# More buffers for edge loads, dense one-hots and a new dealing of edge sums in a graph network

## The chip, the cores and the metric

The kernel runs on one core of one Trainium2 chip, in one launch. The time is device microseconds (us) of that core for one execution, inputs and outputs in the chip's memory (DRAM). A time is the median of several runs. The profile comes from one execution of its own.

## What is computed

Two layers of a graph network over 6,250 nodes with 128 features and 200,000 edges that are sorted by their destination:

```python
edge_index = jnp.stack([src, dst])
h = jnp.maximum(_layernorm(x, axis=-1), 0.0)
# layer 0
agg_src = jax.ops.segment_sum(h[src], dst, num_segments=N_NODES)
agg_edge = jax.ops.segment_sum(edge_features, dst, num_segments=N_NODES)
x = x + relu(concatenate([h, agg_src, agg_edge], axis=1) @ W.T + b)
# layer 1: two mean aggregations
h = jnp.maximum(_layernorm(x, axis=-1), 0.0)
h = relu(segment_mean(h[src], dst) @ W1_l + b1 + h @ W1_r)
x = x + relu(segment_mean(h[src], dst) @ W2_l + b2 + h @ W2_r)
```

(segment_mean stands for the sum of the messages divided by the larger of the number of edges and 1.) All inputs and outputs are float32.

## The kernel before

The kernel never gathers a node's row by its index. It first **builds** a dense matrix of counts, how often node s is the source of an edge into node d, as bfloat16 in DRAM (counts_d). Then each of the three aggregations is a dense product of that matrix with the node features. The features go in as three bfloat16 terms that sum to the float32 value (terms). The change lies in the build alone.

**Groups, tiles, units.** The 200,000 edges are cut in 196 groups (G) of 1,024: 128 partitions by U = 8 tiles. Since the edges are sorted by destination, a group touches a narrow window of destination nodes, and since the destinations are drawn unevenly, the window widens as the groups go on. REGIONS holds 14 rows for 14 groups each (RUN): tiles per unit n (4, 2 or 1), nodes of a unit's window w, groups per stretch k, nodes of a ring sw, and nodes of a group's window for the edge sums win (8 to 74). Two regions have n = 4 (28 groups), four have n = 2 (56 groups), eight have n = 1 (112 groups). A **unit** is n tiles that share one window.

**Counts.** For each group VectorE makes two kinds of one-hot matrices in onehots (L391): sp, one column per source's place in its block of 128, and sq, one column per pair of destination in the window and source block (NB = 49 blocks, so NB*w columns). Each has two buffers (pool hots). PE multiplies them tile by tile into a PSUM tile pu (L534), which has three buffers. For n = 1 a second, small matmul (L546) with the one-hot sc adds the tile before, where windows overlap. ScalarE then evicts each unit from pu into a ring in SBUF (L561 for n = 1; L556 and L566 for n > 1), at a place that it reads from a register. For n > 1 GpSimd adds the first 49 columns of a unit into the ring (L564). When a stretch of groups is done, SP writes the ring to counts_d (L584). Three rings take turns.

**Edge sums.** The same groups also give agg_edge. edge_sums(g) has SP load the group's edge features, 512 KB (edge_t, L426, pool edges with 3 buffers). VectorE makes a one-hot hot (L428) of win columns for each of 8 tiles, in one of three padded buffers whose rows are 128 wide. PE multiplies each tile of features with the 128 columns of that row (L437) into a PSUM tile pe with two buffers. VectorE adds the first win columns into aggE at the group's first node (L442), which it reads into a register. The matmuls are float32, and the trace has two PE passes for each.

**The order of the work.** PE's order is written out. After each unit or pair of units of counts, sum_edges lets the edge tiles run up to a place, and a manual dependency puts the next edge matmul behind the counts before it:

```python
spent += share(n) * len(units) / len(live)
sum_edges(min(int(spent / shares * GU + 0.5), GU), counted)
```

share(n) is the weight of a group of counts; GU = 1568 edge tiles are dealt in proportion to it. SP takes all loads and most stores of the build in one queue, in the order that the program gives: edge loads, chunks of x for the layer norm (x_c, L476), rows of the first product (r_d, L352), and the writes of the ring (L584). A load for which no buffer is free, or a write whose ring is not complete, holds up all that stands behind it. Every third group the first layer norm and product of one block of 128 nodes (first_layer, L341 to L351) is fitted in.

Of the kernel before, what the change touches and what calls it, by code (L numbers as in the profile page):

```python
# [9 lines left out]
F32 = mybir.dt.float32  # L10
# [10 lines left out]
P = 128  # L21
D = 128
U = 8
# [29 lines left out]
WINMAX = 74  # L53
# [3 lines left out]
def kernel(ctx: ExitStack, tc: tile.TileContext, x, srcl, dstl, edge, w0t, b0, w1l, b1, w1r, w2l, b2, w2r, out):  # L57
# [11 lines left out]
    nc = tc.nc  # L69
# [55 lines left out]
    build = ExitStack()  # L125
# [47 lines left out]
    for key, t in [*pick.items(), *pick_l.items()]:  # L173
        n = key if isinstance(key, int) else key[0]
        e = 16 * n
# [186 lines left out]

    rings = build.enter_context(tc.tile_pool(name="rings", bufs=1))
    hots = build.enter_context(tc.tile_pool(name="hots", bufs=2))
    edges = build.enter_context(tc.tile_pool(name="edges", bufs=3))

    ring_of = [rings.tile([P, SWMAX * NB], BF16, name=f"ring{i}") for i in (2, 1)]

    padded = [rings.tile([P, U, P], F32, name=f"hot{i}") for i in range(2)]
    ring_of.append(rings.tile([P, SWMAX * NB], BF16, name="ring0"))  # L370
    padded.append(rings.tile([P, U, P], F32, name="hot2"))
    ring_of.reverse()
    padded.reverse()
    for t in ring_of[:1] + padded + ring_of[1:]:
# [3 lines left out]
    def value(ap, engine, most):  # L378
        return nc.values_load(
            ap, engines=[engine], min_val=0, max_val=most, skip_runtime_bounds_check_because="clamped on the chip"  # L380
        )
# [39 lines left out]
    def edge_sums(g):  # L421

        win = win_of(g)
        e = edges.tile([P, U, D], F32, name="edge_t")
        at_e = min(g * EG, E - EG)
        nc.sync.dma_start(e, edge[at_e : at_e + EG, :].rearrange("(p u) f -> p u f", u=U))  # L426
        hot = padded[g % len(padded)]
        nc.vector.tensor_tensor(  # L428
            hot[:, :, :win],
            iota[:, :win].unsqueeze(1).to_broadcast([P, U, win]),  # L430
            rel[:, g, :].unsqueeze(2).to_broadcast([P, U, win]),
            op=ALU.is_equal,
        )
        ps = bpsum.tile([P, 512], F32, name="pe", bufs=2)
        for u in range(U):
            behind = yield
            mm = nc.tensor.matmul(ps[:, :P], e[:, u, :], hot[:, u, :], start=u == 0, stop=u == U - 1)  # L437
            if behind is not None:
                tc.add_manual_dep(mm.ins, behind.name, IN_ORDER, reason="in turn with the counts")
        base = value(first_i[0:1, g : g + 1], ET.DVE, N - 1)  # L440
        to = aggE[:, bass.ds(base, win)]
        nc.vector.tensor_tensor(to, to, ps[:, :win], op=ALU.add)  # L442

    def all_edge_sums():
        for g in range(G):
            yield from edge_sums(g)
# [37 lines left out]
        return products(0, b, h, terms[0], pu[:, :P], pu[:, 512 : 512 + 2 * D], nc.sync)  # L484


    share = lambda n: 1.0 if n > 1 else 2.0
    shares = sum(share(n) * ng for _, ng, n, *_ in stretches)
    spent = 0.0
    before = None  # L490
# [5 lines left out]
    for si, (g0, ng, n, w, k, sw, win) in enumerate(stretches):  # L496
# [7 lines left out]
        for g in range(g0, g0 + ng):  # L504
# [21 lines left out]
            for j in range(0, len(live), many):  # L526
                units = live[j : j + many]
                pu = bpsum.tile([P, 2 * 512], F32, name="pu", bufs=3)
                for i, t0 in enumerate(units):
                    for t in range(t0, t0 + n):  # L530
                        c = i * 512
                        while c < i * 512 + nq:
                            z = min(c // 512 * 512 + 512, i * 512 + nq)
                            mm = nc.tensor.matmul(  # L534
                                pu[:, c:z],
                                sp[:, t, :],
                                sq[:, t, c - i * 512 : z - i * 512],
                                start=t == t0,
                                stop=t == t0 + n - 1 and (n > 1 or c > i * 512),
                            )  # L540
                            c = z
                    if n == 1:

                        slot = t0 + 1 if t0 != live[0] else 1
                        for j0, (sp_b, t) in enumerate(last_tiles):
                            mm = nc.tensor.matmul(  # L546
                                pu[:, i * 512 : i * 512 + NB],
                                sp_b[:, t, :],
                                sc[:, slot + 1 - len(last_tiles) + j0, :NB],
                                start=False,  # L550
                                stop=j0 == len(last_tiles) - 1,
                            )
# [207 lines left out]
    for b in order:  # L760
# [10 lines left out]
        n = P if b + 1 < NB else last  # L771
# [231 lines left out]
```

## Time and profile before

| | us |
|---|---|
| median of 3 runs | 2244.61 (2238.09 to 2248.94) |
| the profiled execution | 2237.15 |
| its span | 2235.4 |
| PE busy in the span | 2073.7 (93%) |
| VectorE busy | 1242.0 (56%) |
| ScalarE busy | 789.2 (35%) |
| GpSimd busy | 205.0 (9%) |
| groups of counts with n = 4 | from 34 us |
| with n = 2 | from 106.5 us |
| with n = 1 | from 310.5 us |
| end of the build | 911.5 us |

In the rows of the profile PE is the tensor engine's matmuls, PEld its weight loads, DVE VectorE, ACT ScalarE, POOL GpSimd, SP SyncE; a q behind a name is the engine's sequencer, which issues, loads registers and waits. L437 is line 437 of the kernel. A row of a group reads: line, engine, operation, tile written <- tiles read, shape, xcount | busy us in all, mean ns of one | idle us of the engine just before them <- what ended most of it. A row of waits reads: who <- for whom: us in total, times, longest. A row of the timeline reads: start us, us, engine, line, operation, tiles, xcount [idle before <- releaser]. Matmuls overlap in a pipeline, so the time of a run of them is read from the start of the first to the start of the next instruction. The granted clock is the share of full speed that PE was given.

### The profile page before, as it was taken

What the parts mean: (1) busy time and instruction counts of PE and PEld (TensorE: products, weight loads), DVE (VectorE), ACT (ScalarE), POOL (GpSimd) and SP (SyncE); (2) the same over time, 40 slices, a digit from 0 to 9 for tenths busy, and PEclk for the clock granted to TensorE, in tenths of its full rate; (3) what the DMA queues carried; (4) which work ended last, traced back from release to release, by engine and by line L of the source; (5) the groups of instructions that cost most, each with busy time, mean ns of one, the idle gap of its engine ahead of it and who ended that gap; (6) DMA issues with size and microseconds to landing.
All of it is one profiled execution on the core that took longest, in us unless ns stands there. A gap on an engine that the chain in (4) does not pass through costs nothing.

```text
span 2235.4 us, 38803 instructions
## 1 busy us (share of the span) xinstructions
PE 2073.7 (93%) x13717; PEld 1691.1 (76%) x13717; DVE 1242.0 (56%) x2419; ACT 789.2 (35%) x2011; POOL 205.0 (9%) x427
## 2 busy tenths in 40 slices
PE   6977778899999999689999999999999999999998
PEld 5865567677776677478878887788888888888887
DVE  8987776577777777465555554544444431111111
ACT  3465566688888889211111111111111110000000
POOL 4576650000000000100000000000000000000000
PEclk9999999999999999899999999999999999999999
DMA  3555566678888778745555555555555556666663
GB/s 121 179 191 173 193 221 233 217 266 280 281 301 300 283 293 291 280 167 205 205 194 203 206 205 189 190 194 206 192 190 201 202 187 227 226 226 227 227 226 135
DMA packets 147226, 488.20 MB, mean 218 GB/s; under 512 B 16017, under 2 KB 86735, under 8 KB 127312
## 3 DMA queue, kind: packets, MB, share of 16 engines
q1 hardware_dynamic: 88452, 456.84, 56.9%
q10 hardware_dynamic: 57996, 27.16, 4.2%
q8 instruction: 111, 1.82, 0.3%
q0 software_dynamic: 576, 1.63, 0.2%
q14 instruction: 91, 0.75, 0.1%
HBM read 362.19 MB, written 123.38 MB: 217 GB/s over the span
## 4 chain that ended last, share of the span: by engine, by line
PE 60%; ACT 13%; DMA 9%; DVE 8%; issue 6%; ACTq 2%; POOLq 0%; SPq 0%; POOL 0%; DVEq 0%
PE ps L609 44%; ACT ring L561 10%; PE pe L437 6%; PE pu L534 5%; DMA counts_d<-ring 4%; DMA c<-counts_d 3%; PE pz L344 2%; ACTq L384 1%; DMA edge_t<-in_edge 1%; DVE sq L391 1%; DVE worse L618 1%; PE pt L341 1%; DVE high L617 1%; ACT h L334 1%; DVE sp L391 1%
## 5 line engine op out<-in xcount | busy, mean ns | idle before, releaser
L609 PE MATMUL ps<-terms,c 128*128 128x384 bf16 (+1 forms) x7203 | 1226.7, 327 | 16.9 <-DMA c<-counts_d 16.9
L609 PEld LDWEIGHTS <-c 128*128 128x128 bf16 x7203 | 1019.9, 142 | 183.6 <-issue 21.7
L437 PE MATMUL pe<-hot,edge_t 128*128 128x128 f32 x3136 | 521.0, 294 | 33.5 <-DMA edge_t<-in_edge 17.1
L561 ACT CAST ring<-pu 128x490 f32 (+6 forms) x891 | 469.5, 534 | 96.9 <-PE pu L546 43.0
L437 PEld LDWEIGHTS pe<-hot,edge_t 128*128 128x128 f32 x3136 | 418.2, 195 | 70.2 <-issue 18.1
L534 PE MATMUL pu<-sq,sp 128*128 128x512 bf16 (+7 forms) x1782 | 387.0, 313 | 55.9 <-ACT ring L561 26.7
L391 DVE TENSOR_TENSOR sq<-iota,q_e 128x3136 bf16<-128x3136 f16 (+8 forms) x196 | 353.5, 1804 | 102.4 <-PE pu L546 83.2
L620 DVE TENSOR_REDUCE y<-ps 128x128 f32<-128x384 f32 x147 | 81.2, 552 | 383.3 <-PE ps L609 383.3
L534 PEld LDWEIGHTS <-sp 128*128 128x128 bf16 x1782 | 175.6, 100 | 99.4 <-issue 33.6
L564 POOL TENSOR_TENSOR ring<-ring,fore 128x49 f32 x280 | 161.8, 578 | 102.3 <-ACT fore L556 36.1
L618 DVE TENSOR_REDUCE worse<-high 128x1 f32<-128x3136 bf16 x49 | 167.5, 3419 | 1.6
L546 PE MATMUL pu<-sc,sp 128*128 128x49 bf16 x892 | 163.1, 186 | 0.0
L347 DVE TENSOR_TENSOR r<-pz,b_sb 128x128 f32<-128x128 f32 x98 | 28.6, 292 | 225.0 <-ACT terms L345 225.0
L391 DVE TENSOR_TENSOR sp<-iota,p_e 128x1024 bf16<-128x1024 f16 x196 | 135.4, 691 | 21.8 <-PE pu L534 16.9
L546 PEld LDWEIGHTS <-sp 128*128 128x128 bf16 x892 | 87.0, 98 | 70.2 <-issue 38.5
L566 ACT CAST ring<-pu 128x196 f32 (+5 forms) x280 | 112.3, 403 | 67.9 <-issue 39.5
L330 ACT ACTIVATE rstd<-mv,eps 128x1 f32<-128x1 f32 x98 | 29.5, 301 | 291.1 <-DVE mv L328 291.0
L757 ACT ACTIVATE h<-y 128x128 f32<-128x128 f32 x49 | 15.2, 309 | 281.0 <-DVE y L749 281.0
L617 DVE TENSOR_TENSOR high<-c 128x3136 bf16<-128x3136 bf16 x49 | 87.6, 1789 | 42.1 <-DMA c<-counts_d 42.1
L428 DVE TENSOR_TENSOR hot<-iota,rel 128x64 f32<-128x64 f16 (+13 forms) x196 | 96.5, 493 | 0.0
L351 DVE TENSOR_TENSOR terms<-z,terms 128x128 bf16<-128x128 f32 x147 | 43.9, 299 | 59.5 <-ACT terms L350 59.0
L350 ACT CAST terms<-z 128x128 bf16<-128x128 f32 x147 | 44.0, 299 | 76.4 <-DVE z L349 75.6
(144 smaller groups left out, 867.3 us busy)
## 6 DMA issues: line engine op xcount, KB each, us to landing
c<-counts_d SPq DMA_DIRECT2D x147, 1568.0 KB, 6.1
edge_t<-in_edge SPq DMA_DIRECT2D x196, 512.0 KB, 4.2
counts_d<-ring SPq DMA_DIRECT2D x21, 735.0 KB, 3.8
counts_d<-ring SPq DMA_DIRECT2D x14, 1004.5 KB, 5.4
counts_d<-ring SPq DMA_DIRECT2D x14, 931.0 KB, 4.7
counts_d<-ring SPq DMA_DIRECT2D x14, 882.0 KB, 4.6
counts_d<-ring SPq DMA_DIRECT2D x14, 833.0 KB, 4.9
own<-r_d ACTq DMA_DIRECT2D x147, 64.0 KB, 5.3
```

The lines of the kernel that those rows point to most:

```text
L391: nc.vector.tensor_tensor(to.rearrange("p t (c two) -> p t c two", two=2), iota[:, :m].rearrange("p (c two) -> p c two", two=2).unsqueeze( ...
L428: nc.vector.tensor_tensor(hot[:, :, :win], iota[:, :win].unsqueeze(1).to_broadcast([P, U, win]), rel[:, g, :].unsqueeze(2).to_broadcast([P ...
L437: mm = nc.tensor.matmul(ps[:, :P], e[:, u, :], hot[:, u, :], start=u == 0, stop=u == U - 1)
L534: mm = nc.tensor.matmul(pu[:, c:z], sp[:, t, :], sq[:, t, c - i * 512 : z - i * 512], start=t == t0, stop=t == t0 + n - 1 and (n > 1 or c ...
L546: mm = nc.tensor.matmul(pu[:, i * 512 : i * 512 + NB], sp_b[:, t, :], sc[:, slot + 1 - len(last_tiles) + j0, :NB], start=False, stop=j0 == ...
L561: nc.scalar.copy(ring[:, bass.ds(to_put[t0], nq)], pu[:, i * 512 : i * 512 + nq])
L564: add = nc.gpsimd.tensor_tensor(to, to, fore[:, i, :], op=ALU.add)
L566: put = nc.scalar.copy(ring[:, bass.ds(to_put[t0 // n] + NB, nq - NB)], pu[:, i * 512 + NB : i * 512 + nq])
L609: nc.tensor.matmul(ps[:, :m], stands, moves, start=i == 0, stop=i == len(products) - 1)
L617: nc.vector.tensor_tensor(high, cf[:, :half], cf[:, half:], op=ALU.max)
L618: nc.vector.tensor_reduce(worse[:, 6 + b : 7 + b], high, AX.X, ALU.max)
L620: nc.vector.tensor_reduce(y, ps[:, : NK * D].rearrange("p (k f) -> p f k", k=NK), AX.X, ALU.add)
```

## The change

Three things change in the build.

1. The pool of the edge loads has five buffers in place of three.
2. The one-hots for the edge sums are written close together: tile u stands at column u*win in place of u*128. A matmul still reads 128 columns; those past its own win belong to the next tile, and the sums in them are not used, as only the first win columns of the result are added to aggE. A buffer shrinks from 1,024 to 646 float32 columns.
3. The weights by which edge tiles are dealt to the groups of counts are 1.0, 1.5 and 1.75 for units of four, two and one tiles, in place of 1.0, 1.0 and 2.0.

```diff
-    edges = build.enter_context(tc.tile_pool(name="edges", bufs=3))
+    edges = build.enter_context(tc.tile_pool(name="edges", bufs=5))
...
-    padded = [rings.tile([P, U, P], F32, name=f"hot{i}") for i in range(2)]
+    HP = U * WINMAX + P - WINMAX
+    HP += HP % 2
+    padded = [rings.tile([P, HP], F32, name=f"hot{i}") for i in range(2)]
     ring_of.append(rings.tile([P, SWMAX * NB], BF16, name="ring0"))
-    padded.append(rings.tile([P, U, P], F32, name="hot2"))
+    padded.append(rings.tile([P, HP], F32, name="hot2"))
...
         nc.vector.tensor_tensor(
-            hot[:, :, :win],
+            hot[:, : U * win].rearrange("p (u w) -> p u w", w=win),
             iota[:, :win].unsqueeze(1).to_broadcast([P, U, win]),
             rel[:, g, :].unsqueeze(2).to_broadcast([P, U, win]),
             op=ALU.is_equal,
...
-            mm = nc.tensor.matmul(ps[:, :P], e[:, u, :], hot[:, u, :], start=u == 0, stop=u == U - 1)
+            mm = nc.tensor.matmul(ps[:, :P], e[:, u, :], hot[:, u * win : u * win + P], start=u == 0, stop=u == U - 1)
...
-    share = lambda n: 1.0 if n > 1 else 2.0
+    share = lambda n: {4: 1.0, 2: 1.5, 1: 1.75}[n]
```

## The prediction

> **What bounds the kernel now.** I read the page's slices first: from 960 us on PE is busy nine tenths and no line of the change runs there. The change acts in the build, which ends at 911.5 us. I cut the build where the number of tiles per unit changes, by the starts of VectorE's one-hots: groups 0 to 27 (units of four) from 34 us, 28 to 83 (units of two) from 106.5, 84 to 195 (units of one) from 310.5; the last stage once more at 463, because two different engines limit its parts, and at 749.5, where a unit's columns no longer fit 512. Columns: stage, length, busy time of PE, weight loads, VectorE, ScalarE, GpSimd, granted clock, DMA share, GB/s.
>
> ```profile
> 34.00:106.50 72.50, 66.04 (x523) 57.91 (x524) 65.37 (x155) 33.33 (x122) 39.36 (x60) 0.95 0.57 186
> 106.50:310.50 204.00, 158.80 (x1077) 124.19 (x1075) 163.75 (x328) 119.22 (x428) 136.53 (x232) 0.96 0.54 186
> 310.50:463.00 152.50, 127.70 (x1038) 107.32 (x1037) 97.91 (x238) 100.00 (x281) 7.74 (x19) 0.96 0.68 233
> 463.00:749.50 286.50, 268.16 (x2086) 204.91 (x2084) 220.88 (x372) 247.95 (x501) 0.20 (x1) 1.00 0.82 289
> 749.50:911.50 162.00, 152.51 (x1245) 115.36 (x1244) 120.33 (x154) 140.57 (x226) 1.77 (x1) 0.99 0.79 287
> ```
>
> In the two-tile stage no engine is full: PE 78%, VectorE 80%, GpSimd 67%. From 463 us PE looks full at 94%, but ScalarE's own timeline says otherwise. Eight evictions take 5.1 us, each batch starts about 0.15 us after the last, and a group lasts 5.25 us:
>
> ```profile
> 795.65 5.09 ACT L561 CAST ring<-pu 128x539 f32 x8 [0.15 <-issue]
> 800.90 5.10 ACT L561 CAST ring<-pu 128x539 f32 x8 [0.16 <-PE pu L546]
> 806.15 5.10 ACT L561 CAST ring<-pu 128x539 f32 x8 [0.15 <-issue]
> ```
>
> So past 463 us the evictions are the bound. What they still wait for, in the table of waits from 463 to 911.5 us, is all that a relieved PE or DMA can give back there, 31 us of 448:
>
> ```profile
> ACT ring L561 <- DMA counts_d<-ring: 15.7, 15, 2.6
> ACT ring L561 <- PE pu L546: 15.1, 24, 1.6
> ```
>
> Next the chain that ended last, cut to the two-tile stage (its listed steps are start, length, what):
>
> ```profile
> 194.33 5.18 DMA edge_t<-in_edge
> ...
> 263.78 5.30 DMA edge_t<-in_edge
> ```
>
> and the same places in PE's timeline, with one at 318 to 324 us and one at 392 to 398 us, and an undisturbed run of eight edge matmuls for comparison:
>
> ```profile
> 178.59 0.77 PE L437 MATMUL pe<-hot,edge_t 128*128 128x128 f32 x2 [3.36 <-DMA edge_t<-in_edge]
> ...
> 199.56 0.79 PE L437 MATMUL pe<-hot,edge_t 128*128 128x128 f32 x2 [3.08 <-DMA edge_t<-in_edge]
> ...
> 269.22 2.05 PE L437 MATMUL pe<-hot,edge_t 128*128 128x128 f32 x8 [5.22 <-DMA edge_t<-in_edge]
> ...
> 323.94 0.91 PE L437 MATMUL pe<-hot,edge_t 128*128 128x128 f32 x6 [3.50 <-DVE st L326]
> ...
> 397.69 0.77 PE L437 MATMUL pe<-hot,edge_t 128*128 128x128 f32 x2 [3.23 <-DMA edge_t<-in_edge]
> ...
> 704.39 1.14 PE L437 MATMUL pe<-hot,edge_t 128*128 128x128 f32 x8
> ```
>
> Five times PE stands for 3 to 5 us for a late edge tile (18.4 us in sum; at 323.94 the label names VectorE, but the two edge loads had only been issued at 318.5 and 319.9). The loads are late because SP is one queue: in the two-tile stage its counts writes (L584) waited 65.8 us for GpSimd's last ring add, and the edge loads stand behind them, at most three buffers ahead.
>
> **Five buffers.** The five stalls go, 18.4 us of PE idle. After each, the trace shows the clock halved: eight edge matmuls took 2.05 us after the 5.22 us stall against 1.14. Counting the slow work behind each, about 2 us more per stall, 10 in all. A rule bears on this: the Trainium skill, "TensorE: Matmul & The Clock Gate", HAM oscillation, says that idle gaps above some 3.4 us put PE at half clock. By the rule only the 5.22 and the 3.50 us stalls would cost (4 us of slow work, as an estimate); by the rows the 3.08 and 3.23 us ones did as well. I take the rows: 10.
>
> In the built order SP's edge loads run 5 to 7 tiles ahead of PE instead of 3 to 5. In groups 112 to 194 each counts write stands behind an edge load whose buffer comes free on average 28 PE instructions (weight loads counted) after the group's last matmul; before it was 40. So the ring is written out earlier, and the 15.7 us of ring waits should shrink, not grow.
>
> **Shares.** 28, 56 and 112 groups have units of four, two and one. The weights summed to 28 + 56 + 224 = 308; now to 28 + 84 + 196 = 308. So the first stage keeps its 17.8 edge groups of 196, the second goes from 35.6 to 53.5, the last from 142.5 to 124.7: 17.8 edge groups move. Each is 16 PE passes (two for each float32 matmul). Eight took 0.97 us at 704.39, the next count matmul starting at 705.36: 1.94 us a group, 34.6 us of PE work moved. On VectorE each brings a one-hot and an add,
>
> ```profile
> L428 DVE TENSOR_TENSOR hot<-iota,rel 128x176 f32<-128x176 f16 x13 | 4.9, 393 | 0.0
> L442 DVE TENSOR_TENSOR aggE<-aggE,pe 128x22 f32 x10 | 1.7, 168 | 0.5 <-PE pe L437 0.5
> ```
>
> 0.56 us, 10.0 us in all. The 17.8 moved edge loads are 9.3 MB, 46 GB/s more over 204 us: 232, below the 289 that the later stage sustains.
>
> Two-tile stage. PE's busy time becomes 158.8 + 34.6, less 6 of slow clock (three of the stalls are here), 187. How full PE can run is unknown here. The bounds are the neighbours: 84% as at 310 to 463 us, which still has stalls, and 94% as after 463: 223 or 199 us. I take 87%, what the 310 stage has once its two stalls (6.7 us) and slow clock are taken out of both sides ((127.7 - 4) / (152.5 - 6.7 - 4)): 215 us, **+11**, stalls already credited. VectorE is then at 174 of 215, not the bound. The aggE add stands in VectorE's queue ahead of the next groups' sp and sq and waits for PE's last edge matmul; it waited 26.8 us for 109 sums after 463 us, 0.25 us each, so 4 us for 17.8 more, inside the 87%.
>
> 310 to 463 us. A quarter of the moved groups, 4.45 x 1.94 = 8.6 us of PE, and 4 of slow clock go: 115 us of PE at 87% is 132. ScalarE's work (100 us and its register loads) is then near; I take 135, **-17** (bounds 132 and 142, the stalls alone).
>
> 463 to 911.5 us. The remaining 26 us of PE work are taken out of a stage that ScalarE paces, so nearly all of it becomes PE idle. Of the 31 us of waits I take 12: half the waits for PE, under a third of those for the ring. **-12**, bounds 0 and -25. If evictions did not cover it, the full 26 would return.
>
> The first stage and all that follows the build are as before: 0.
>
> **Dense one-hots.** The write keeps its element count. Matmuls now read 128 columns from row starts at multiples of 4 x window bytes, not 512. The count one-hots already start each tile 588 bf16 columns, 1176 bytes, after the last, no multiple of 512 either, and four of their matmuls of 441 columns pass in 0.91 us, of which one alone is 0.36: 183 ns each, 2.4 columns a ns: taken as 0. Bound above: 4 ns on each of 3136, 12 us. The three memsets of L375 shrink by 378 columns before the first one-hot, some 1 us, beside the first edge load, for which PE waits until 38.5 us.
>
> A rule speaks against the move: the Trainium skill, "SBUF — State Buffer", Who interferes with whom: a VectorE instruction with two SBUF inputs holds the port that GpSimd reads through, and the other blocks for the whole instruction. The moved one-hots have two SBUF inputs and enter the stage where GpSimd adds into the ring (L564). By the rule, 17.8 x 0.39 = 7 us more for GpSimd. The trace has L564 at 273 ns when alone and up to 1.9 us beside sq, which agrees; beside a hot alone four of them took 270 to 282 ns, which does not. I take 0 here and leave the 7 to a rival.
>
> **Sum.** +11 - 17 - 12 = -18. The profiled execution took 2237.15 us (span 2235.4), so 2219; the median of the runs is 2244.61, 7.5 more, and I put the change on that: **2227**.
>
> **Rivals.** A change of 0.5%, 11 us, is about what a measurement of this kernel can tell from none: below 2233 is faster, above 2256 slower.
>
> *ScalarE gives nothing back.* If after 463 us only 3 us return, since evictions pace the stage, the 310 stage stops at -12 because ScalarE fills up there too, and two tiles cost +13, the sum is -2: 2243, no change. For it: batches 0.15 us apart. Against: the 31 us of listed waits and the stalls.
>
> *The two-tile stage pays in series (slower).* PE runs in a written order, so an added edge tile stands between a unit's matmuls and the next unit. If the rounds PE, ScalarE, GpSimd, VectorE leave no room, PE's 34.6, VectorE's 10 and the port's 7 add up: 51.6, less 9 for the stalls (half of the stage's 11.7 idle and 6 slow, as the other engines use such time), +43, against -29 later: +14, 2259. For it: 45 us of PE idle there, much of it waits for ring evictions, in gaps of 1 to 2 us. Against: eight more passes fit in 1 us. It decides from a stage length of 233 us (204 + 29).
>
> **How the numbers follow.** Forecast 0.63, its own range 2207 to 2233 (the bounds above, not all at one end); nothing back 0.20; in series 0.15; dense reads that cost 0.02. Under 2200 all three terms would have to reach their best bound (-5 - 21 - 25), and above 2256 the series case holds most: low 2200, high 2256. Faster 0.65, same 0.20, slower 0.15.
>
> **What would show it.** Right: edge matmuls of 17.8 groups more between the starts of groups 28 and 84; no PE idle above 2.5 us behind an edge load and fewer half-clock stretches; two-tile stage near 215 us, units of one near 572 in place of 601; ScalarE's waits for PE and ring after 463 us near 19 us. Wrong: two tiles at 230 or more; group periods after 463 us unchanged; stalls of PE that now name VectorE or GpSimd in place of the load; edge matmuls above 0.97 us for eight.

## The result, and the profile after

The changed kernel takes **2222.22 us** (median of 5 runs, 2206.9 to 2225.29) against 2244.61 before (2238.09 to 2248.94): the ratio is 0.9895, 95% interval 0.9871 to 0.9920, some 22 to 24 us faster. The forecast was 2227 us, faster.

The profiled execution of the changed kernel took 2206.9 us, its span 2205.2. That is the fastest of its five runs, so its span is 30 us shorter than before, not 22 to 24. The stages were cut at the same groups as before, 28, 84 and 112, and once more at 168 (the columns are those of the prediction's first fence):

```profile
34.00:106.40 72.40, 65.90 (x523) 57.83 (x524) 65.36 (x155) 33.38 (x122) 39.26 (x60) 0.95 0.61 199
106.40:307.00 200.60, 181.86 (x1356) 153.05 (x1355) 170.13 (x357) 120.85 (x428) 137.92 (x230) 0.99 0.68 233
307.00:445.40 138.40, 118.94 (x989) 99.32 (x988) 98.48 (x238) 102.19 (x285) 9.83 (x22) 0.96 0.73 252
445.40:727.80 282.40, 253.44 (x1928) 187.05 (x1927) 216.80 (x353) 243.96 (x498) 0.20 (x1) 1.00 0.76 273
727.80:884.50 156.70, 148.65 (x1173) 106.08 (x1172) 117.61 (x146) 140.05 (x228) 1.77 (x1) 1.00 0.75 278
```

Read the second line against the one before: 279 more PE matmuls in the two-tile stage and 23 us more of PE busy time, in a stage that is 3.4 us *shorter*, at 99% of the clock in place of 96%. GpSimd's busy time is as it was, 138 us. DMA moved 233 GB/s there (forecast 232).

The chain of work in that stage has no step on an edge load any more; its longest steps are:

```profile
144.86 2.57 issue
171.83 2.12 ACTq L387
210.89 2.46 PE pe L440 x22
293.90 2.24 ACTq L387
301.98 2.07 issue
```

After group 112, the table of waits has for ScalarE:

```profile
ACT ring L564 <- PE pe L440: 11.3, 13, 1.4
ACT ring L564 <- PE pu L549: 10.1, 15, 1.5
...
ACT ring L564 <- DMA counts_d<-ring: 5.9, 10, 1.7
```

The waits for the ring fell from 15.7 to 5.9 us. Those for PE did not fall, they rose from 16 to 21 us. And a new long stop stands in PE's timeline at the start of the units of one, while the chain of groups 84 to 111 shows a chunk of x for the layer norm, issued at 318.8 us (first line the chain, second PE):

```profile
318.82 5.79 DMA x_c<-in_x
```

```profile
327.64 0.40 PE L537 MATMUL pu<-sq,sp 128*128 128x294 bf16 x1 [6.37 <-ACT ring L564]
```

### The profile page after: what moved, and what is told of

Its sections match the earlier page's. It is cut to its first block, busy times and chain, and to the rows that moved or that the text cites. A ratio compares the mean times of both kernels' runs of the same rounds, so it can differ in the third digit from the quotient of the medians.

```text
span 2205.2 us, 38759 instructions
## 1 busy us (share of the span) xinstructions
PE 2068.5 (94%) x13717; PEld 1684.8 (76%) x13717; DVE 1242.1 (56%) x2419; ACT 788.0 (36%) x2011; POOL 208.3 (9%) x427
## 4 chain that ended last, share of the span: by engine, by line
PE 62%; ACT 14%; issue 7%; DVE 6%; DMA 6%; ACTq 2%; POOLq 1%; POOL 0%; DVEq 0%; SPq 0%
PE ps L612 47%; ACT ring L564 11%; PE pe L440 6%; PE pu L537 5%; DMA counts_d<-ring 3%; PE pz L344 2%; ACTq L387 2%; DMA c<-counts_d 1%; PE pt L341 1%; DVE worse L621 1%; ACT h L334 1%; DVE high L620 1%; DVE sq L394 1%; ACT ring L569 1%; PE pu L344 1%
## 5 line engine op out<-in xcount | busy, mean ns | idle before, releaser
L440 PE MATMUL pe<-hot,edge_t 128*128 128x128 f32 x3136 | 514.4, 291 | 4.5 <-issue 2.2
L394 DVE TENSOR_TENSOR sp<-iota,p_e 128x1024 bf16<-128x1024 f16 x196 | 135.8, 693 | 14.5 <-PE pu L537 11.0
```

The costliest lines, as they stand in the source:

```text
L394: nc.vector.tensor_tensor(to.rearrange("p t (c two) -> p t c two", two=2), iota[:, :m].rearrange("p (c two) -> p c two", two=2).unsqueeze( ...
L440: mm = nc.tensor.matmul(ps[:, :P], e[:, u, :], hot[:, u * win : u * win + P], start=u == 0, stop=u == U - 1)
```

## The experiments

Two theories stood at the start. The first is the prediction's: late edge loads cost PE time, PE's idle time in the two-tile stage takes the moved sums, and after group 112 evictions on ScalarE pace. The other: one part alone makes the gain. Stage lengths below come from one profiled execution of each kernel; the kernel times of four runs (all sums out of the two-tile stage, all into it, spare additions, spare copies) are one execution each too. Three kernels with five buffers and the new weights (the changed one, the one with padded rows, the one with early chunks of x) had 200.6, 207.8 and 209.8 us in the two-tile stage, so a difference under some 9 us in that stage is not taken for an effect.

### Each part alone

Five buffers and dense one-hots, the old weights:

```diff
-    share = lambda n: {4: 1.0, 2: 1.5, 1: 1.75}[n]
+    share = lambda n: 1.0 if n > 1 else 2.0
```

> Five edge buffers and dense one-hots, with the old weights (1.0, 1.0, 2.0). Theory (two parts that each pay: the late edge loads cost PE idle and slow clock, and the units of one are relieved by the move): the five stalls behind edge loads go, 10 to 18 us faster than before, ratio 0.992 to 0.996, with the two-tile stage at 186 to 196 us (204 before) and the stage from there to the end of the build 3 to 12 us shorter than 601. Rival (the gain is the move alone, PE's idle time at the stalls is covered by GpSimd and ScalarE): within 4 us of before, two-tile stage above 200 us.

2236.35 us against 2240.94 of the kernel before on that chip: ratio 0.9977 (0.9964 to 0.9990), 5 us faster, less than the theory's 10 to 18 and just over the rival's 4. Stages from group 28, from 84 and from 112 to the end of the build:

```profile
106.10:310.80 204.70, 157.73 (x1076) 123.47 (x1074) 163.16 (x325) 119.98 (x427) 135.18 (x228) 0.97 0.54 185
310.80:456.40 145.60, 123.97 (x1042) 104.42 (x1042) 99.06 (x243) 100.36 (x281) 10.79 (x24) 0.99 0.71 245
456.40:909.20 452.80, 422.51 (x3326) 321.95 (x3323) 339.98 (x524) 388.79 (x728) 1.98 (x2) 0.99 0.80 284
```

No PE stop above 1.4 us behind an edge load is left among groups 28 to 83, and the stage still takes 204.7 us, as before the change (204.1). So the three stalls that the kernel before had there, 11.7 us of PE idle plus slow clock, cost its stage nothing that shows: the rival was right for this stage. Groups 84 to 111 became 7 us shorter (145.6 against 152.9), so there the theory was. From group 112 on the stage was 5 us longer (452.8 against 448.1).

The new weights and dense one-hots, three buffers:

```diff
-    edges = build.enter_context(tc.tile_pool(name="edges", bufs=5))
+    edges = build.enter_context(tc.tile_pool(name="edges", bufs=3))
```

> The new weights and dense one-hots with three edge buffers. Theory: half as many edge groups more are wanted per unit of time in the two-tile stage, where SP's queue holds the loads back, so with three buffers PE stalls more often there: more than three stalls above 2.5 us behind an edge load between groups 28 and 84, a stage of 212 to 235 us, and what the later stages give (about 25 us) is mostly eaten: between 10 us faster and 10 us slower than before. Rival (the move alone makes the gain): 18 to 25 us faster, as the whole change, with a two-tile stage near 201 us.

2231.49 us, ratio 0.9957 (0.9943 to 0.9970), 10 us faster, at the good end of the theory's range. The two-tile stage grew to 219.6 us:

```profile
105.80:325.40 219.60, 185.75 (x1358) 155.34 (x1357) 171.21 (x363) 121.69 (x429) 137.78 (x243) 0.97 0.65 222
```

PE's timeline shows stops like these in it:

```profile
234.17 0.68 PE L440 MATMUL pe<-hot,edge_t 128*128 128x128 f32 x4 [3.39 <-DMA edge_t<-in_edge]
```

```profile
311.86 1.41 PE L440 MATMUL pe<-hot,edge_t 128*128 128x128 f32 x5 [5.13 <-DMA edge_t<-in_edge]
```

There were fewer stops above 2.5 us behind an edge load than expected, these two (the stage ends at 325.4), and four of 1.6 to 2.4 us. At the new weights two more buffers are worth 10 to 19 us of the stage's length. Groups 84 to 111 took 130.6 us, 22 less than before, and the stage from 112 on 443, 5 less.

Only the dense one-hots (both edits above undone):

> Only the dense one-hots; three buffers and the old weights. Theory: no difference, within 4 us of before, eight edge matmuls in a row in 0.97 us. Rival (reads of rows that start at odd places cost PE time): 3136 passes at 2 to 4 ns more, 6 to 12 us slower; eight matmuls above 0.985 us.

2249.61 us, ratio 1.0040 (1.0024 to 1.0056): 9 us *slower*. Theory and rival both miss in part. The reads are not at fault: the median distance of two edge passes that follow each other was 112 ns in every stage, as before the change. But PE waited 28.0 us for edge loads from group 28 to 111, where the kernel before had 16.5 us under that name, and with waits as long as

```profile
189.89 0.77 PE L440 MATMUL pe<-hot,edge_t 128*128 128x128 f32 x2 [6.88 <-DMA edge_t<-in_edge]
```

The two-tile stage took 212.1 us and groups 84 to 111 157.9 (204.1 and 152.9 before). The layout also alters the order of the built program: on VectorE the second hot stands ahead of an sp, behind which it stood before, and in SP's queue 20 of the 586 transfers stand at another place, all between 161 and 302 us. This explains the stop shown. PE waited there for the 34th edge load, which in the kernel before was issued ahead of a write of the ring, and here behind it and 9 us later (two lines of SP before, then two of this kernel):

```profile
175.30 0.45 SPq L426 DMA_DIRECT2D edge_t<-in_edge  x1
...
181.74 0.35 SPq L584 DMA_DIRECT2D counts_d<-ring  x1
```

```profile
184.12 0.35 SPq L587 DMA_DIRECT2D counts_d<-ring  x1
184.56 1.35 SPq L429 DMA_DIRECT2D edge_t<-in_edge  x2
```

How much of the 9 us such stops make is not shown: the two-tile stage alone is not further from 204.1 us than like kernels are from each other.

This run changes how the two before it are read, for both have the dense layout. Measured from here, five buffers bring 0.63% (1.0040 to 0.9977), the new weights 0.83% (to 0.9957), and the whole change 1.45% (to 0.9895): they add up. Measured from the kernel before, 0.23% and 0.43% make less than 1.05%. The new weights with three buffers and padded rows were not run, so whether the parts need each other, or the layout's 0.40% was only in the way of both, stays open.

Five buffers and the new weights, but padded one-hots:

```diff
-            hot[:, : U * win].rearrange("p (u w) -> p u w", w=win),
+            hot[:, :, :win],
...
-            mm = nc.tensor.matmul(ps[:, :P], e[:, u, :], hot[:, u * win : u * win + P], start=u == 0, stop=u == U - 1)
+            mm = nc.tensor.matmul(ps[:, :P], e[:, u, :], hot[:, u, :], start=u == 0, stop=u == U - 1)
```

> Five buffers and the new weights, one-hots in padded rows of 128 as before. Theory: the dense layout costs and gives nothing, so the time is that of the whole change, 18 to 25 us faster than before. Rival (the dense layout takes part in the gain, or costs): more than 5 us away from the changed kernel.

2219.07 us, ratio 0.9900 (0.9875 to 0.9925): the whole gain, without the dense layout. With five buffers no difference of the layout can be told (0.9895 with it), and the five buffers do not need the memory that it frees.

### What paces the two-tile stage

Next all edge sums were taken out of the two-tile stage, then all put into it. The weights were chosen so that the first stage keeps its share.

```diff
-    share = lambda n: {4: 1.0, 2: 1.5, 1: 1.75}[n]
+    share = lambda n: {4: 1.0, 2: 0.0, 1: 2.5}[n]
```

> The changed kernel with weights 1.0, 0.0, 2.5: no edge tile is dealt to the 56 groups with units of two, all 53.5 edge groups of theirs go to units of one; the first stage keeps its 17.8. Theory (the two-tile stage is paced by the round of ScalarE and GpSimd, its edge sums lie in PE's idle time): the stage stays at 190 to 201 us although PE loses about 104 us of work. Rival (the stage is paced by PE's sums): it falls to 100 to 170 us. For the units of one both expect growth: 53.5 x 1.94 = 104 us more of PE work, 60 to 105 us of time.

```profile
105.80:311.90 206.10, 129.37 (x518) 65.19 (x516) 152.53 (x262) 119.84 (x428) 133.07 (x228) 0.77 0.26 97
```

With 518 matmuls in place of 1356, 14 edge passes in place of 853, a quarter of the DMA's time in use, the stage takes 206.1 us, 5 above the theory's range and far above the rival's. It is paced by something that the edge sums do not touch, and up to the changed kernel's share they are free there. (The kernel as a whole took 2263.11 us, 29 more than the one before: the 53.5 edge groups now stand among the units of one. These grew by some 54 us, less than the 60 to 105 that both expected.)

ScalarE and GpSimd were the candidates. Each was given more work that nobody reads:

```diff
                     add = nc.gpsimd.tensor_tensor(to, to, fore[:, i, :], op=ALU.add)
                     tc.add_to_no_dep_group(f"add{si}", add.ins)
+                    spare = small.tile([P, NB], BF16, name="spare", bufs=2)
+                    nc.gpsimd.tensor_tensor(spare, fore[:, i, :], fore[:, i, :], op=ALU.add)
```

> The changed kernel with one more GpSimd addition beside each ring add of units of two and four, into a spare tile that nobody reads: some 224 more in the two-tile stage, 0.27 us each alone, about 0.58 as measured beside VectorE's one-hots. Theory (GpSimd is one of the engines that pace the two-tile stage): it grows by 45 to 130 us. Rival (GpSimd has slack there, 138 us busy of 201): it grows by less than 20 us.

```profile
106.90:363.80 256.90, 203.81 (x1358) 166.56 (x1356) 174.07 (x363) 124.00 (x429) 202.84 (x454) 0.90 0.53 183
```

```diff
+                    again = small.tile([P, 2, NB], F32, name="fore_again", bufs=2)
+                    nc.scalar.copy(
+                        again[:, : len(units), :], pu.rearrange("p (i c) -> p i c", c=512)[:, : len(units), :NB]
+                    )
```

> The changed kernel with ScalarE's copy of each pair of units' first columns made twice, the second into a tile that nobody reads: 112 more of 0.25 us in the two-tile stage, 28 us of ScalarE work. Theory (ScalarE's chain of register loads and copies paces the two-tile stage): it grows by 18 to 30 us. Rival (ScalarE, 121 us busy of 201, has slack): it grows by less than 8 us.

```profile
106.10:307.40 201.30, 180.64 (x1355) 152.72 (x1354) 169.69 (x353) 134.71 (x538) 128.55 (x232) 0.99 0.66 229
```

GpSimd's busy time rose by 65 us and the stage by 56. ScalarE made 111 more copies, 29 us in all (its busy time rose by 14 only, since the records of successive instructions overlap), and the stage did not move; the kernel took 2212.0 us. So more GpSimd work lengthens the stage and more ScalarE copies do not: of the theory that named both engines, the half on ScalarE fell.

How can an engine pace that is 68% busy? Its register loads are not in the busy time. The row of these loads in GpSimd's queue, kernel before, two-tile stage (count, then shortest, median, longest ns):

```profile
L384 POOLq TENSOR_LOAD <-at_i x53: 495/950/1894, 108.4 to 304.9; - x53
```

The stage's 75 loads (these, and 22 at the seams, where one ring takes over from another) take 70 us. Of these, 31 run beside an addition that has not ended, so that loads and instructions together fill 176 of the 204 us. The rest is short: 229 gaps of at most 0.35 us, most of them under 0.1 us, make 26 us, and only four gaps are longer, 2.4 us in all. The longer gaps are read here as waiting for other engines, the short ones as the step from one instruction to the next. The same account of six traces (us):

| two-tile stage | length | GpSimd busy or loading | gaps up to 0.35 us | longer gaps |
|---|---|---|---|---|
| before | 204.1 | 175.7 | 26.1 | 2.4 |
| after | 200.6 | 172.8 | 24.4 | 3.5 |
| no edge sums | 206.1 | 173.1 | 26.5 | 6.5 |
| spare GpSimd additions | 256.9 | 236.0 | 17.9 | 3.0 |
| three buffers, new weights | 219.6 | 180.8 | 26.5 | 12.3 |
| all edge sums (below) | 398.9 | 160.2 | 7.1 | 231.5 |

So GpSimd was full already before the change. Where PE paces, in the last row, most of the stage is long gaps. ScalarE, counted in the same way, has 17 us of longer gaps after the change: it is not far from full, but not full.

Half of the additions' time is not GpSimd's own. Before the change the 212 additions took 587 ns on average; the 48 that ran beside no VectorE instruction took 273 ns at the median, and those that began within a VectorE sq up to 1.93 us. No run took the sq away, so how far the stage would fall without them is open.

A try to relieve it failed, and says the same. GpSimd loads the places for two groups at once:

```diff
-                to_add = group_values(places, ET.Pool, (sw - w) * NB)
+                several = 2 if n == 2 else 1
+                at_g = (g - g0) % several
+                if at_g == 0:
+                    m_g = min(several, g0 + ng - g)
+                    of_several = group_values(at_i[0:1, g * U : (g + m_g) * U : n], ET.Pool, (sw - w) * NB)
+                to_add = of_several[at_g * (U // n) : (at_g + 1) * (U // n)]
```

> The changed kernel, but GpSimd loads the places of its ring adds into registers once for two groups with units of two in place of once a group: 26 fewer loads of 1.2 us, some 30 us of GpSimd's time in the two-tile stage; its additions and ScalarE's loads stay. Theory (GpSimd's additions and loads together pace the stage): the stage falls by 8 to 25 us, the kernel is 5 to 20 us faster than the changed one. Rival (the loads are hidden behind the additions' waits): the stage stays within 4 us of 201.

```profile
L387 POOLq TENSOR_LOAD <-at_i x30: 495/3494/4562, 108.5 to 335.8; - x30
```

2230.25 us, ratio 0.9981 (0.9971 to 0.9992), slower than the changed kernel. The loads fell from 53 to 30, but one of eight places takes 3.5 us where one of four took 0.95: together 87 us in place of 63. The stage grew by 31 us to 232.0:

```profile
106.60:338.60 232.00, 193.86 (x1357) 160.07 (x1356) 171.17 (x363) 122.66 (x429) 130.33 (x234) 0.94 0.59 203
```

GpSimd's instructions and loads fill 206 us of it, 33 more than in the changed kernel, short gaps 25 and longer gaps 1. Neither expectation held, since both took a load's price as fixed. GpSimd's account still explains the stage.

### What the units of one can give back

```diff
-    share = lambda n: {4: 1.0, 2: 1.5, 1: 1.75}[n]
+    share = lambda n: {4: 1.0, 2: 5.0, 1: 0.0}[n]
```

> The changed kernel with weights 1.0, 5.0, 0.0: no edge tile among the units of one, 178 edge groups in the two-tile stage. It measures what the units of one take without any edge sum. Theory (after group 112 ScalarE's evictions pace): from group 112 to the end of the build 405 to 425 us, where the changed kernel took 439 and the one before 448, although PE loses 194 us of work there; groups 84 to 111 in 115 to 130 us (138). Rival (PE paces): below 330 us. The two-tile stage grows to 400 to 460 us by PE's sum.

```profile
105.60:504.50 398.90, 391.89 (x3289) 368.55 (x3288) 258.88 (x625) 135.28 (x431) 138.94 (x244) 1.00 0.85 282
504.50:629.40 124.90, 94.82 (x555) 58.42 (x554) 82.20 (x157) 101.82 (x277) 4.21 (x7) 0.67 0.33 131
629.40:1050.20 420.80, 290.62 (x1597) 142.38 (x1596) 269.43 (x310) 374.79 (x726) 1.98 (x2) 0.79 0.43 173
```

The kernel took 2375.24 us. Without any edge sum the units of one need 124.9 + 420.8 us, where the changed kernel has 138.4 + 439.0 and the one before 152.9 + 448.1. After group 112, 27 us are all that could ever be had; the change took 9 of them. ScalarE paces there, as forecast: its instructions and register loads fill 390 of the 420.8 us, gaps of at most 0.35 us 30, and longer gaps 0.8. The two-tile stage with 178 edge groups took 399 us, PE 98% busy, just under what PE's sum gave.

As much moved once more:

```diff
-    share = lambda n: {4: 1.0, 2: 1.5, 1: 1.75}[n]
+    share = lambda n: {4: 1.0, 2: 2.0, 1: 1.5}[n]
```

> The changed kernel with weights 1.0, 2.0, 1.5: 71.3 edge groups in the two-tile stage, 106.9 among the units of one, as much again as the change moved. Theory (GpSimd paces the two-tile stage at 200 to 206 us whatever PE does, and PE alone would need about 192 us for it by the rate of the kernel with all sums before the units of one): the stage stays at 200 to 210 us and the units of one give another 5 to 10 us: 3 to 10 us faster than the changed kernel, ratio to before 0.985 to 0.989. Rival (the two-tile stage was already full of PE work at 91% busy): the stage grows by 20 to 35 us and the kernel is 10 to 25 us slower than the changed one.

2215.46 us, ratio 0.9916 (0.9893 to 0.9938): no gain over the changed kernel. The two-tile stage and the stage from group 112 on:

```profile
105.50:316.10 210.60, 205.62 (x1623) 181.48 (x1623) 179.66 (x402) 122.45 (x430) 137.65 (x234) 1.00 0.75 262
...
447.70:895.40 447.70, 390.63 (x2891) 272.26 (x2889) 327.25 (x469) 381.61 (x727) 1.98 (x2) 0.98 0.68 254
```

PE was busy for 205.6 of 210.6 us (the theory had counted on 192), so it is full there and GpSimd no longer alone. Groups 84 to 111 gave 7 us more, but from 112 on 447.7 us were needed, 9 more than in the changed kernel, with 13 sums fewer (443.3 in the kernel with padded rows). The table of waits has ScalarE wait for PE for 31 us there, 10 more than in the changed kernel, but such a row also counts the time in which ScalarE loads registers. Its 85 loads took 74 us, against 65 in the changed kernel and 55 before; gaps above 0.35 us that hold neither a load nor an instruction rose only from 5 to 8 us. So 6 of the 9 us are ScalarE's own loads and instructions. Why the loads became longer stays open.

### The new stop behind a chunk of x

```diff
-        xc = edges.tile([P, XB, D], F32, name="x_c", bufs=2)
+        xc = edges.tile([P, XB, D], F32, name="x_c", bufs=3)
...
-            load_chunk(b // XB + 1)
+            load_chunk(b // XB + 2)
...
-    for i in range(2):
+    for i in range(3):
```

> The changed kernel with three buffers for the chunks of x and each chunk asked for one chunk earlier. Theory: the stall of 6.4 us that the changed kernel shows at 321 us, behind a chunk of x that was issued at 318.8 us, goes with its slow clock (10 us at half): 4 to 10 us faster than the changed kernel, groups 84 to 111 in 128 to 134 us in place of 138. Rival (ScalarE and the ring set this stage, and the chunk only holds up what has time): within 3 us of the changed kernel.

```profile
106.70:316.50 209.80, 183.40 (x1358) 153.90 (x1357) 171.16 (x357) 122.13 (x429) 142.83 (x233) 0.98 0.64 222
316.50:446.40 129.90, 116.27 (x984) 97.53 (x983) 99.72 (x243) 101.37 (x283) 8.21 (x19) 0.99 0.76 268
446.40:883.00 436.60, 402.50 (x3103) 293.62 (x3100) 332.89 (x490) 383.91 (x725) 1.98 (x2) 1.00 0.74 276
```

2203.37 us against 2234.87 on that chip, ratio 0.9859 (0.9832 to 0.9886), the fastest of all. Groups 84 to 111 took 129.9 us as the theory said, and the stop is gone (the longest PE gap there is 2.2 us). Against the changed kernel the step is 0.4%, but the two ratios were measured beside different runs of the kernel before and their intervals overlap: likely, not certain.

At last the joined loads and the early chunks, by the edits above, and with them

```diff
-    share = lambda n: {4: 1.0, 2: 1.5, 1: 1.75}[n]
+    share = lambda n: {4: 1.0, 2: 2.0, 1: 1.5}[n]
```

> Weights 1.0, 2.0, 1.5, GpSimd's loads once for two groups with units of two, and the chunks of x earlier. Theory: GpSimd would need some 175 us in the two-tile stage, PE about 192 us and paces it: 190 to 205 us, with 5 to 10 us less among the units of one: 10 to 22 us faster than the changed kernel, ratio to before 0.979 to 0.985. Rival (what one gives, the next takes, as PE is now short everywhere): within 5 us of the changed kernel.

2242.28 us, ratio 1.0030 (1.0016 to 1.0043), slower than the kernel before. The two-tile stage took 228.0 us, so neither expectation held; the joined loads do the harm that they do alone, and the other two edits do not make up for it.

## Why the prediction was right, and where it was not

**The sum.** -18 us forecast, -22 by the medians. Its parts by the profiles: two tiles +11 forecast, -3 measured (+4 to +6 in the two sister kernels with other one-hots or chunks); groups 84 to 111 -17 forecast, -14.5 measured; from 112 on -12 forecast, -9; what lies outside 0 forecast, -3. The likeliest case came true, and the series case (two tiles at 233 us or more) did not. That the sum came so near is in part luck: the first term was 14 us too high, the next two 2.5 and 3 us too hopeful, and the profiled gain is 30 us where the medians have 22. Among groups 84 to 111 the gain is ScalarE's waiting: its gaps above 0.35 us that hold no register load fell from 32 to 14.5 us.

**"In the two-tile stage no engine is full" failed.** With its register loads and the short gaps about them GpSimd was full: its longer gaps made 2.4 us of 204. The step that took PE's fullness from the neighbouring stage, 87%, and so 215 us, is the one that was mis-sized: PE ran 91% busy in 200.6 us, since up to GpSimd's own 200 to 206 us its work is free. The bounds given, 199 and 223, held.

**The five stalls were real, their price was not.** Their idle time and slow clock were credited with their full length inside the 87%. At the old weights, taking them away gave the two-tile stage nothing (204.7 us). They cost 7 us among groups 84 to 111. At the new weights, where PE's work fills GpSimd's pace, late loads cost more: three buffers made the two-tile stage 10 to 19 us longer than five, and GpSimd's longer gaps, 12 us, were 3 to 4 in the kernels with five.

**Evictions pace after 463 us: right.** ScalarE's gaps above 0.35 us without a load in them fell from 18 to 5 us from group 112 on, so 13 us of true waiting went, about the 12 that were taken. But its register loads, which the prediction held fixed, took 65 us in place of 55; with them ScalarE fills 403 us in place of 399, and 9 us were left. The split was wrong. The waits for PE, of which half were to go, grew by 5 in the table, which counts a load's time too. The ring's waits fell by 10 us, more than the third that was taken, and not through the five buffers, under which the prediction has them: five buffers alone leave them as they were, and the new weights alone halve them (first line five buffers, second line new weights):

```profile
ACT ring L564 <- DMA counts_d<-ring: 16.3, 17, 2.4
```

```profile
ACT ring L564 <- DMA counts_d<-ring: 7.5, 7, 1.7
```

**Dense one-hots at 0: right for the change**, as the padded kernel shows; the 4 ns bound was never approached. Alone, with three buffers, they cost 9 us. They changed the order of SP's queue and with it made loads later, which the prediction had not thought of; how much of the 9 us that is stays open.

**The rule that spoke against the move** (the Trainium skill, "SBUF — State Buffer", Who interferes with whom) was given 0. In the kernel without edge sums in the two-tile stage, GpSimd was busy 133 us against 138 with 53 more one-hots, and its instructions and loads together filled 173 us in both. So at most 5 us lie with them, where the rule's blocking would make some 20, as an estimate, of 53 one-hots of 0.39 us. In the kernel before, 28 additions began while such a one-hot ran, and 25 of them took at most 0.29 us, as if alone. The moved third of the one-hots cost GpSimd nothing that can be told.

**Clock gate.** The rows were chosen over the rule's 3.4 us. The granted clock was one half after each of the five stops, those of 3.08 and 3.23 us too. Nothing later spoke against the choice: in the kernel without sums in the two-tile stage PE had the clock at 77%, with only two idle gaps above 3.1 us in 206 us.

## What to carry to other kernels

An engine whose queue loads registers can be full at 68% busy: before it is called idle, lay the loads of its sequencer over its instructions (overlaps counted once) and see what gaps are left, and give it a little useless work to see whether the stage grows. Work that is moved into a stage which another engine paces is free only as long as its inputs come in time, so deal out the work and deepen the prefetch together; and run each part alone, the one that should do nothing too, since here it cost 0.4% by itself and may have hidden part of what the others gave. Once one stop in a queue is gone, look at the next load in the same queue; here it was the chunk of x.

## What the runs showed that was not expected

A GpSimd load of four places into registers took 0.95 us at the median, one of eight 3.5 us, so that one load for two groups costs more than one for each. The number alone does not set the price: ScalarE loads eight places that lie side by side in 0.55 us at the median among the units of one, where those of GpSimd lie two apart; which difference matters was not tried. And the clock was halved in stretches with no long idle time at all: with no edge sums among the units of one, PE had 79% of the clock from group 112 to the end of the build, and its longest idle gap there was 1.9 us, its busy share 69%.
